# A 7x7 depthwise convolution whose taps are cut to the image, on one Trainium2 core

## Chip, core and metric

The kernel runs on one core of one Trainium2 chip. A core has TensorE (PE, matrix products into PSUM), VectorE (DVE, elementwise work), ScalarE (ACT, activation functions), GpSimd (POOL, here it issues the DMAs that add while they copy) and SyncE (SP, here it issues plain DMAs). Each engine works through its own queue in order, and they wait for one another by semaphores. The metric is the time of the device in microseconds for the whole program: the median of several executions. Profiles and traces are of one further execution.

## The reference

Eight images of 384 channels and 32 x 32 pixels, all float32, pass through two layers. Cut to what matters here:

```python
# layer 0: a transformer block on 1024 tokens of 384 channels
q, k, v = qkv(layernorm(xf))                       # 8 heads of 48
x1 = proj(softmax(q @ k.T * SCALE) @ v) + xf
x = x1 + fc2(gelu(fc1(layernorm(x1))))             # hidden 1536

# layer 1: a ConvNeXt block
y = conv_general_dilated(x, dw_w, padding=((3, 3), (3, 3)), feature_group_count=384)   # 7x7, depthwise
y = layernorm_over_channels(y + dw_b)
y = gelu(y @ w1 + b1)                              # 384 -> 1536
gx = sqrt(sum(y * y, over the pixels)); nx = gx / (mean(gx) + GRN_EPS)
y = grn_gamma * (y * nx) + grn_beta + y
out = x + y @ w2 + b2                              # 1536 -> 384
```

The depthwise convolution multiplies, for each of the 384 channels, 49 shifted copies of the image by 49 weights and adds them up. Outside the image the shifted copy is zero.

## The kernel before

The 384 channels are three tiles of 128 partitions, and an image of a tile is 1024 elements in each partition. The convolution is no matrix product here: a tap is one VectorE instruction, `acc = window * weight + acc`, on a tile with a border of three zeros all round (38 x 38). While it runs for image b - 1, TensorE is at the attention and the first MLP of image b. In the calls shown, `start_conv(b, ...)` begins the convolution of an image, and `conv_norm`, which runs inside the MLP of the next image, hangs its layer norm behind it.

```python
pad = const.tile([P, CT, HP, WP], F32, name="pad")          # 128 x 3 x 38 x 38, zeros at the border

def inner(ct):
    return pad[:, ct, PAD : PAD + H, PAD : PAD + W]

def convolution(acc, us, first=(), y0=0, y1=H, ready=tuple(range(CT)), taken=None):
    done = [0] * CT
    ct, n = None, 0
    taps = KS * KS - (HELPED if taken is not None else 0)    # HELPED = 7
    while min(done) < taps:
        left = [c for c in ready if done[c] < taps and not (taken and taken.get(c, 0) > flow.now)]
        # ... wait when there is none ...
        ct = min([c for c in left if c != ct] or left, key=lambda c: done[c])
        i = done[ct]
        dy, dx = divmod(i, KS)
        window = pad[:, ct, dy + y0 : dy + y1, dx : dx + W]
        dst = image(acc[:, ct, :])[:, y0:y1, :]
        tap = col("dww", ct * KS * KS + i)
        if i == 0:
            nc.vector.tensor_scalar(dst, window, tap, col("dwb", ct), ALU.mult, ALU.add)      # L978
        else:
            nc.vector.scalar_tensor_tensor(dst, window, tap, dst, ALU.mult, ALU.add)          # L980
        done[ct] += 1
        n += 1
        yield next((early for m, early in first if n <= m), us)
```

Seven of the 49 taps of a tile are taken over by ScalarE, which multiplies half an image at a time, and by GpSimd's DMAs, which add the product to `acc`. Meanwhile VectorE leaves that tile alone (`taken`).

```python
def help_convolution(acc, us, taken):
    yield 8.0
    for ct in reversed(range(CT)):
        taken[ct] = float("inf")
        for i in range(KS * KS - HELPED, KS * KS):
            dy, dx = divmod(i, KS)
            for h in range(2):
                # ... pauses while `quiet` ...
                t = three.tile([P, NH], F32, tag="res", bufs=4, name=f"tap_{ct}_{i}_{h}")
                y0 = dy + h * H // 2
                window = pad[:, ct, y0 : y0 + H // 2, dx : dx + W]
                tap = col("dww", ct * KS * KS + i)
                nc.scalar.mul(t.rearrange("p (h w) -> p h w", w=W), window, tap)              # L1001
                nc.gpsimd.dma_start(out=acc[:, ct, half(h)], in_=t, accum_op=ALU.add)         # L1002
                yield us
        taken[ct] = flow.now + 8.0
```

The order of the instructions is settled when the program is built. A small scheduler, `Flow`, counts how much time TensorE's matmuls should take (0.857 us for one of 512 columns) and, as that count passes, lets the other chains (convolution, layer norms, helpers) put their next instruction in their queues. What a chain yields is the number of such microseconds until its next step. So `us` is the pace at which taps are put among the other VectorE instructions, and `first` gives other paces for the first taps.

```python
start_conv(b, 1.65 if b == B - 2 else 1.7, (26, 2.2), (27, 9.0), (35, 4.4))     # in the loop; image 0: 1.6, (9, 1.65), (17, 4.4)
```

The last image has nothing left to hide behind, so it is split. Its MLP goes by halves of the image, and its convolution, which has no helpers and writes into the place of `wqkv`, starts on rows 0 to 12 when half of the image is ready, and then does rows 13 to 31:

```python
conv = convolution(last, 0.86 if h else 0.66, (), *rows, ready[h])
```

A layer norm over channels sums three tiles on VectorE, folds the two halves of the partitions with an adding DMA, sums over partitions with a matrix of ones on TensorE (the result stays in a PSUM bank), and subtracts the mean on VectorE, which frees the bank. The banks of this kind are four, in turn:

```python
ps_o = ctx.enter_context(tc.tile_pool(name="ps_o", bufs=4, space=PSUM))

# in layernorm(), cut:
nc.vector.tensor_tensor(a, src[:, 0, cols], src[:, 1, cols], ALU.add)                         # L413
nc.vector.tensor_tensor(a, a, src[:, 2, cols], ALU.add)                                       # L416
totals = yield from token_sums(a, ...)                                                        # L388 DMA; L380 or L394 matmul
nc.vector.scalar_tensor_tensor(to, total, -1.0 / C, of, ALU.mult, ALU.add)                    # L423, for each tile
# ... squares on ScalarE, summed (L434, L437) and added over partitions in the same way,
#     rstd by Ln (L447) and Exp (L448) on ScalarE ...
nc.vector.scalar_tensor_tensor(dst[:, ct, cols], dst[:, ct, cols], col(g, ct), rstd, ALU.mult, ALU.mult)   # L451
```

Of the kernel before, what the change touches and what calls it, by code (L numbers as in the profile page):

```python
# [52 lines left out]
B, C, H, W = 8, 384, 32, 32  # L53
# [6 lines left out]
KS, PAD = 7, 3  # L60
# [7 lines left out]
HELPED = 7  # L68
# [83 lines left out]
def block_kernel(  # L152
# [32 lines left out]
    def half(h):  # L185
        return slice(h * NH, (h + 1) * NH)
# [22 lines left out]
    pad = const.tile([P, CT, HP, WP], F32, name="pad")  # L209
# [14 lines left out]
    def col(name, i):  # L224
        at, width = VEC[name]
        assert i < width
        return vec[:, at + i : at + i + 1]

    def inner(ct):
        return pad[:, ct, PAD : PAD + H, PAD : PAD + W]  # L230

    def image(ap):
        return ap.rearrange("p (h w) -> p h w", h=H)
# [562 lines left out]
    def mlp(b, xt, xn, weights, tag, ln, rest, before_fc2=None, behind_ln=None):  # L796

        hid = one.tile([P, HT * N], F32, tag="big", name=f"hid_{b}").rearrange("p (m n) -> p m n", m=HT)
        e = [three.tile([P, 2, NH], F32, tag="p", name=f"fc2_e_{b}_{i}") for i in range(2)]
        wa = f"fc1_{tag}"  # L800
        flow.finish(ln)
        for m in range(HT):
            gelu_half(hid, m, 0, xn, weights, wa, f"fc1_{b}")
            if m == 3 and rest:
                rest()
                slow = 1.2 if b == 1 else 1.0
                ln = flow.spawn(layernorm(xt, xn, 1, eps0, "g2", f"ln2_{b}", True, slow=slow))
                behind_ln(ln)
        flow.finish(ln)
        for m in range(HT):  # L810
            gelu_half(hid, m, 1, xn, weights, wa, f"fc1_{b}")
            if m % CM == CM - 1:
                weights.used(wa, m // CM)
            if m in (3, 5):
                two_tiles = hid[:, m - 3 : m - 1, :]
                difference(e[(m - 3) // 2], two_tiles[:, :, half(0)], two_tiles[:, :, half(1)])
        if before_fc2:
            before_fc2()
        bias = lambda r: col("bfc2", r)
        by_thirds(xt, hid, e, True, weights, f"fc2_{tag}", bias, lambda r, n: pad_half(xt, r, n), f"fc2_{b}")  # L820
# [132 lines left out]
    def keep(b, xt):  # L953

        kept = dram.tile([C, N], F32, tag="kept", name=f"kept_{b}")
        nc.sync.dma_start(out=kept.rearrange("(c p) n -> p c n", p=P), in_=xt)
        return kept

    def convolution(acc, us, first=(), y0=0, y1=H, ready=tuple(range(CT)), taken=None):

        done = [0] * CT
        ct, n = None, 0
        taps = KS * KS - (HELPED if taken is not None else 0)
        while min(done) < taps:
            left = [c for c in ready if done[c] < taps and not (taken and taken.get(c, 0) > flow.now)]
            if not left:
                yield 1.0
                continue  # L970
            ct = min([c for c in left if c != ct] or left, key=lambda c: done[c])
            i = done[ct]
            dy, dx = divmod(i, KS)
            window = pad[:, ct, dy + y0 : dy + y1, dx : dx + W]
            dst = image(acc[:, ct, :])[:, y0:y1, :]
            tap = col("dww", ct * KS * KS + i)
            if i == 0:
                nc.vector.tensor_scalar(dst, window, tap, col("dwb", ct), ALU.mult, ALU.add)  # L978
            else:
                nc.vector.scalar_tensor_tensor(dst, window, tap, dst, ALU.mult, ALU.add)  # L980
            done[ct] += 1
            n += 1
            yield next((early for m, early in first if n <= m), us)

    def help_convolution(acc, us, taken):

        yield 8.0
        for ct in reversed(range(CT)):
            taken[ct] = float("inf")
            for i in range(KS * KS - HELPED, KS * KS):  # L990
                dy, dx = divmod(i, KS)
                for h in range(2):
                    if quiet:
                        while quiet:
                            yield 1.0
                        yield 3.0
# [9 lines that stand above are left out]
        taken.clear()  # L1006
# [188 lines left out]
    def load_kept(b, kept):  # L1195
        t = one.tile([P, CT, N], F32, tag="x", name=f"kept_{b}")
        nc.sync.dma_start(out=t, in_=kept.rearrange("(c p) n -> p c n", p=P))
        return t
# [13 lines left out]
    def after(first, chain, us=0):  # L1212
        if us:
            yield us
        while first is not None and first.gi_frame is not None:
            yield 1.0
        yield from chain
# [202 lines left out]
    def main():  # L1420
# [46 lines left out]
        def start_conv(b, us, *first):  # L1467
            acc = state["acc"] = one.tile([P, CT, N], F32, tag="acc", name=f"acc_{b}")
            taken = {}
            state["conv"] = flow.spawn(convolution(acc, us, first, taken=taken), paced=True)  # L1470
            state["help"] = flow.spawn(help_convolution(acc, 2.7, taken), paced=True)
# [53 lines left out]
        for b in range(B):  # L1525
            if b == 0:
                folding = flow.spawn(after(None, folds(weights), 8))
                preparing = flow.spawn(after(None, prepare(weights, False), 4))
                aside = flow.spawn(after(folding, prepare(weights, True), 4))
            q_and_k = qk(b, state["xn"], weights if b else None)  # L1530
            ln2, rest, xn = attention(b, xt, *q_and_k, (folding, aside) if b == 0 else ())
            if b < B - 1:
                mlp(b, xt, xn, weights, b, ln2, rest, lambda: next_norms(b), lambda ln: conv_norm(b, ln))
            else:
                acc = state["acc"]
                mlp_by_halves(b, xt, xn, weights, ln2, rest, last_convolution)
            kept[b] = keep(b, xt)
            if b + 1 < B:
                acc = state["acc"]
            if b == 0:  # L1540
                xt = load_x(b + 1, "x")
                flow.finish(preparing)
                start_conv(b, 1.6, (9, 1.65), (17, 4.4))
                next_values(1)
                continue
            if b < B - 1:
                xt = load_kept(b - 1, kept.pop(b - 1))
            flow.finish(state["norm3"])
            if b < B - 1:
                y, gx = grn_up(b - 1, acc, weights, b - 1)  # L1550
                start_conv(b, 1.65 if b == B - 2 else 1.7, (26, 2.2), (27, 9.0), (35, 4.4))
                scale = flow.spawn(grn_scale(b - 1, gx, weights, b - 1, y))
                next_values(b + 1)
                flow.finish(scale)
                quiet.append("w2")
                grn_down(b - 1, y, xt, weights, b - 1, b - 1)
                quiet.clear()
                xt = load_x(b + 1, "x")
            else:

                norm_b = flow.spawn(after(state["conv"], last_norm(LAST[1], 1.0)))
                norm_c = flow.spawn(after(norm_b, last_norm(LAST[2], 1.2)))
                y, gx = grn_up_straight(b - 1, acc, weights, b - 1)
                scale = flow.spawn(grn_scale(b - 1, gx, weights, b - 1))
                flow.finish(state["norm_a"])
                sums = small.tile([P, CT, HT], F32, tag="gx_last", bufs=1, name="gx_last")
                y_last = places()
                last_up(last, y_last, 0, sums, weights)
                flow.finish(scale)
                halves = lambda k, part: y[:, k, part]  # L1570
                blocks = [(r, half(n)) for r in range(CT) for n in range(2)]
                args = b - 1, halves, kept[b - 1], weights
                grn_down_straight(*args, b - 1, b - 1, blocks[:-1])
# [147 lines left out]
```

## Time and profile before

| | |
|---|---|
| time, median of 3 | 3316.8 us (3315.48 to 3319.44) |
| span of the profiled execution | 3315.9 us, 38765 instructions |
| TensorE busy | 3279.8 us |
| VectorE busy | 2511.5 us |
| ScalarE busy | 1604.1 us |
| taps of images 0 to 6 on VectorE | 861 at 1276 ns, and 21 first taps at 807 ns |
| taps of image 7 on VectorE | 144 at 644 ns and 144 at 844 ns, and 6 first taps |
| taps on ScalarE | 294 at 727 ns |

The profile gives each engine's busy time and the idle time ahead of its instructions, with what ended it (`<-` and the releaser). A wait view sums those by pair, a timeline puts the instructions in order of time, and a view by stretches gives busy time and the granted TensorE clock (1.00 is full speed) for any stretch. Each 32-bit product shows as two matmul records, so two passes of 512 columns make one product of the kernel.

### The profile page before, as it was taken

What the parts mean: (1) busy time and instruction counts of PE and PEld (TensorE: products, weight loads), DVE (VectorE), ACT (ScalarE), POOL (GpSimd) and SP (SyncE); (2) the same over time, 40 slices, a digit from 0 to 9 for tenths busy, and PEclk for the clock granted to TensorE, in tenths of its full rate; (3) what the DMA queues carried; (4) which work ended last, traced back from release to release, by engine and by line L of the source; (5) the groups of instructions that cost most, each with busy time, mean ns of one, the idle gap of its engine ahead of it and who ended that gap; (6) DMA issues with size and microseconds to landing.
All of it is one profiled execution on the core that took longest, in us unless ns stands there. A gap on an engine that the chain in (4) does not pass through costs nothing. (4 is left out here: it accounts for less than half of the span.)

```text
span 3315.9 us, 38765 instructions
## 1 busy us (share of the span) xinstructions
PE 3279.8 (99%) x14296; PEld 1415.0 (43%) x14296; DVE 2511.5 (76%) x3186; ACT 1604.1 (48%) x2194; POOL 484.2 (15%) x569
## 2 busy tenths in 40 slices
PE   8999999999999999999999999999999999999998
PEld 4344434443344433444344443444434443444455
DVE  4444897888867978679786798768886888879940
ACT  2542663447534375353652737526473355623541
POOL 2121210112110121101211022111220112100000
PEclk9999999999999999999999999999999999999999
DMA  5336732657244563537436373273742647333231
GB/s 197 112 106 147 150 68 71 156 115 150 56 104 135 137 127 58 131 106 172 84 58 148 103 187 70 58 179 84 175 78 50 180 106 160 63 74 89 69 95 43
DMA packets 199109, 368.73 MB, mean 111 GB/s; under 512 B 40768, under 2 KB 46784, under 8 KB 198528
## 3 DMA queue, kind: packets, MB, share of 16 engines
q0 software_dynamic: 80896, 158.63, 26.3%
q1 hardware_dynamic: 117728, 206.83, 20.7%
q8 instruction: 115, 1.88, 0.2%
q10 hardware_dynamic: 288, 0.71, 0.1%
q14 instruction: 82, 0.67, 0.1%
HBM read 187.03 MB, written 34.60 MB: 67 GB/s over the span
## 5 line engine op out<-in xcount | busy, mean ns | idle before, releaser
L980 DVE SCALAR_TENSOR_TENSOR acc<-pad,vec,acc 128x1024 f32<-128x1024 f32 x861 | 1069.3, 1276 | 20.1 <-DMA acc<-tap 15.5
L673 ACT ACTIVATE p<-s 128x1024 f32<-128x1024 f32 x512 | 523.8, 1023 | 278.5 <-PE s L664 270.1
L664 PE MATMUL s<-qk 48*64 48x512 f32 x4096 | 544.7, 593 | 0.8 <-ACT p L673 0.6
L684 PE MATMUL o<-p,v 64*64 64x512 f32 x4096 | 541.2, 591 | 0.0
L351 PE MATMUL fc<-xn,fc 128*128 128x512 f32 x1152 | 504.0, 596 | 4.8 <-DVE acc L423 4.8
L1002 POOL DMA_DIRECT2D acc<-tap x294 | 253.7, 884 | 1212.2 <-ACT tap L1001 747.9
L351 PEld LDWEIGHTS fc<-xn,fc 128*128 128x128 f32 x1152 | 219.2, 191 | 285.6 <-issue 275.7
L358 PE MATMUL fc_p<-hid,fc 128*128 128x512 f32 x728 | 318.6, 594 | 0.2 <-DMA hid<-hid 0.2
L370 ACT ACTIVATE hid<-fc,bfc_f 128x512 f32<-128x512 f32 x192 | 131.5, 686 | 348.0 <-PE fc L351 347.6
L684 PEld LDWEIGHTS o<-p,v 64*64 64x64 f32 x4096 | 165.5, 133 | 278.3 <-issue 266.7
L664 PEld LDWEIGHTS s<-qk 48*64 48x64 f32 x4096 | 161.2, 133 | 278.6 <-issue 220.5
L358 PE MATMUL o_p<-y,w 128*128 128x512 f32 x624 | 272.3, 593 | 0.0
L1051 DVE TENSOR_TENSOR y<-h,y 128x512 f32<-128x512 f32 x288 | 197.0, 690 | 90.8 <-PE h L358 76.2
L1001 ACT ACTIVATE tap<-pad,vec 128x512 f32<-128x512 f32 x294 | 210.9, 727 | 25.4 <-DMA acc<-tap 25.2
L358 PEld LDWEIGHTS fc_p<-hid,fc 128*128 128x128 f32 x728 | 137.2, 190 | 179.0 <-issue 166.5
L358 PE MATMUL h<-acc,w_A 128*128 128x512 f32 x432 | 207.3, 595 | 0.0
L980 DVE SCALAR_TENSOR_TENSOR wqkv<-pad,vec,wqkv 128x416 f32<-128x416 f32 (+1 forms) x288 | 193.5, 744 | 0.5
L358 PEld LDWEIGHTS o_p<-y,w 128*128 128x128 f32 x624 | 117.5, 190 | 150.6 <-issue 129.1
L790 ACT COPY pad<-x 128x512 f32<-128x512 f32 x48 | 30.2, 635 | 251.0 <-DVE x L856 187.0
L625 DVE TENSOR_TENSOR attn<-o,attn 128x512 f32<-128x512 f32 x64 | 44.1, 689 | 138.6 <-ACT attn L623 138.6
L549 DVE TENSOR_TENSOR qk<-qk,qk 128x512 f32<-128x512 f32 x168 | 111.5, 686 | 29.0 <-PE qk L358 20.0
L592 PE MATMUL v<-wqkv,xn 128*128 128x384 f32 x384 | 128.2, 491 | 0.0
(311 smaller groups left out, 3751.4 us busy)
## 6 DMA issues: line engine op xcount, KB each, us to landing
acc<-tap POOLq DMA_DIRECT2D x294, 256.0 KB, 3.5
w_A<-in_w SPq DMA_DIRECT2D x72, 384.0 KB
fc<-s_fc SPq DMA_DIRECT2D x91, 256.0 KB
hid<-hid POOLq DMA_DIRECT2D x42, 512.0 KB, 7.1
fc<-in_wfc SPq DMA_DIRECT2D x54, 384.0 KB
w<-s_w SPq DMA_DIRECT2D x78, 256.0 KB
y<-y POOLq DMA_DIRECT2D x36, 512.0 KB, 6.8
kept<-x SPq DMA_DIRECT2D x8, 1536.0 KB
```

Source lines behind the costliest of these rows:

```text
L351: nc.tensor.matmul(out=ps, lhsT=lhsT(k), rhs=rhs(k)[:, half(h)], start=(k == 0), stop=(k == nk - 1))
L358: nc.tensor.matmul(out=bank, lhsT=lhsT, rhs=rhs, start=k == 0, stop=k == len(pairs) - 1)
L370: nc.scalar.activation(dst, src, function, **kw)
L549: nc.vector.tensor_tensor(dst, bank, part, ALU.add)
L592: nc.tensor.matmul(out=ps[:, :C], lhsT=xn[:, k, t * P : (t + 1) * P], rhs=wv_sb[:, k, :], start=(k == 0), stop=(k == CT - 1),)
L664: nc.tensor.matmul(out=s[64 * i : 64 * i + 64, j, :], lhsT=kT[64 * j : 64 * j + HD, m, k0 : k0 + 64], rhs=qT[64 * j : 64 * j + HD, m, half ...
L673: nc.scalar.activation(p, s, AF.Exp)
L684: nc.tensor.matmul(out=outs[i][64 * j : 64 * j + 64, :], lhsT=v[keys, t, at : at + 64], rhs=p[keys, j, :], start=(t == 0), stop=(t == KT - 1),
L980: nc.vector.scalar_tensor_tensor(dst, window, tap, dst, ALU.mult, ALU.add)
L1001: nc.scalar.mul(t.rearrange("p (h w) -> p h w", w=W), window, tap)
L1002: nc.gpsimd.dma_start(out=acc[:, ct, half(h)], in_=t, accum_op=ALU.add)
L1051: nc.vector.tensor_tensor(dst, bank, part, ALU.add)
```

## The change

A tap only touches the part of the output whose source lies inside the image: the others would add zero. For that the first tap, which writes `acc` instead of adding, has to be one that covers the whole image, so the middle tap comes first. The taps on VectorE are cut to their rows and columns. The seven that ScalarE and the adding DMAs take over are now those that lose least by being cut: the one left of the middle and the six others of the middle column. They still work on whole windows with the zero border. So that taps of different size stand at fair distances, the pace is shared out by size (120 elements for the fixed part), with the total as before. Three paces are then set a little faster.

```diff
+    TAPS = [KS * PAD + PAD] + [i for i in range(KS * KS) if i % KS != PAD and i != KS * PAD + PAD - 1]
+    TAPS += [KS * PAD + PAD - 1] + [i for i in range(KS * KS) if i % KS == PAD and i != KS * PAD + PAD]
+
+    def inside(dy, dx, y0, y1):
+        rows = slice(max(y0, PAD - dy), min(y1, H + PAD - dy))
+        return rows, slice(max(0, PAD - dx), min(W, W + PAD - dx))
+
+    def size(dy, dx, y0, y1):
+        rows, cols = inside(dy, dx, y0, y1)
+        return 120 + (rows.stop - rows.start) * (cols.stop - cols.start)
 ...
         taps = KS * KS - (HELPED if taken is not None else 0)
+        shares = [size(*divmod(i, KS), y0, y1) for i in TAPS[:taps]]
+        shares = [taps * s / sum(shares) for s in shares]
 ...
             i = done[ct]
-            dy, dx = divmod(i, KS)
-            window = pad[:, ct, dy + y0 : dy + y1, dx : dx + W]
-            dst = image(acc[:, ct, :])[:, y0:y1, :]
-            tap = col("dww", ct * KS * KS + i)
+            share = shares[i]
+            dy, dx = divmod(TAPS[i], KS)
+            rows, cols = inside(dy, dx, y0, y1)
+            window = inner(ct)[:, rows.start + dy - PAD : rows.stop + dy - PAD, cols.start + dx - PAD : cols.stop + dx - PAD]
+            dst = image(acc[:, ct, :])[:, rows, cols]
+            tap = col("dww", ct * KS * KS + TAPS[i])
 ...
-            yield next((early for m, early in first if n <= m), us)
+            yield share * next((early for m, early in first if n <= m), us)
 ...                                                   # help_convolution
-            for i in range(KS * KS - HELPED, KS * KS):
+            for i in TAPS[KS * KS - HELPED :]:
 ...
-                start_conv(b, 1.65 if b == B - 2 else 1.7, (26, 2.2), (27, 9.0), (35, 4.4))
+                start_conv(b, 1.6 if b == B - 2 else 1.65, (26, 2.1), (27, 9.0), (35, 4.4))
```

## The prediction

> **What bounds the kernel now.** I read the busy shares first, then who waited for whom on TensorE, then the timeline around each TensorE wait, and last the groups of VectorE instructions with their shapes kept apart. The shares, from the page (engine, busy us, share, instructions):
>
> ```profile
> PE 3279.8 (99%) x14296; PEld 1415.0 (43%) x14296; DVE 2511.5 (76%) x3186; ACT 1604.1 (48%) x2194; POOL 484.2 (15%) x569
> ```
>
> TensorE is idle for 3315.9 - 3279.8 = 36.1 us in all. That is a ceiling of 1.1% on what a lighter VectorE (DVE) can return, since the change removes no matmul. A busy TensorE could hide short waits, so I checked one period of the middle: the sums of one image's second layer norm start at 1367.63, 1767.77 and 2167.91 us, 400.14 us apart. A 512-column pass takes 0.429 us in the trace (54 of them in 23.34 us, less the overlapping end of the last), and the matmuls that the program issues between two such points come to 396.2 us at that rate. The other 4 us are some ten switches to and from 64-row tiles at about 0.4 us each (the weight load behind such a switch stands 0.76 us after the one ahead instead of 0.24). So nothing is hidden: in the middle five images TensorE alone sets the pace. The stretches of 400 us say the same (start:end, length, then busy us of each engine, clock, DMA):
>
> ```profile
> 900.00:1300.00 400.00, 399.95 (x1745) 167.03 (x1744) 319.74 (x385) 204.15 (x266) 62.33 (x68) 1.00 0.51 114
> 1300.00:1700.00 400.00, 399.95 (x1745) 166.92 (x1744) 319.75 (x385) 204.16 (x266) 62.34 (x68) 1.00 0.51 114
> ```
>
> TensorE's waits by releaser (us in total, times, longest) are few:
>
> ```profile
> PE ln_sum L380 <- DVE ln_a L416: 11.8, 5, 5.9
> PE fc L351 <- DVE acc L423: 4.8, 1, 4.8
> PE ln_var L380 <- DVE ln_sq L437: 2.4, 1, 2.4
> PE h_last L1150 <- DVE wqkv L451: 1.6, 1, 1.6
> PE ln_var L394 <- DMA ln_sq<-ln_sq: 1.2, 2, 1.0
> ```
>
> By their places: 10.1 us of the first line lie before 30 us, long before the first convolution tap at 334 us. The rest of it (1.7), the 2.4 and the 1.6 lie together at 3183 to 3191 us. About 11 us more are the end after the last large matmul (3304.8 to 3315.9). One wait is left that convolution taps could cause: 4.8 us at 2974.4 to 2979.2. VectorE just ahead of it (start, us, line, operation, out<-in, count, idle before):
>
> ```profile
> 2936.72 15.81 DVE L980 SCALAR_TENSOR_TENSOR acc<-pad,vec,acc 128x1024 f32<-128x1024 f32 x12 [1.72 <-DMA acc<-tap]
> 2952.45 2.07 DVE L451 SCALAR_TENSOR_TENSOR xn<-xn,vec,ln_rstd 128x512 f32<-128x512 f32 x3
> ...
> 2958.54 0.70 DVE L978 TENSOR_SCALAR wqkv<-pad,vec 128x416 f32<-128x416 f32 x1 [0.70 <-ACT pad L790]
> 2959.28 10.28 DVE L980 SCALAR_TENSOR_TENSOR wqkv<-pad,vec,wqkv 128x416 f32<-128x416 f32 x15
> ...
> 2971.55 5.71 DVE L980 SCALAR_TENSOR_TENSOR wqkv<-pad,vec,wqkv 128x416 f32<-128x416 f32 x10
> 2977.17 3.67 DVE L423 SCALAR_TENSOR_TENSOR acc<-ln_sum,acc 128x512 f32<-128x512 f32 x6
> ```
>
> VectorE leaves a DMA wait at 2936.7 and then runs without a real pause: the last 12 taps of image 6 (counted from 0) and the first 27 instructions of image 7's convolution. Only then does it reach the subtraction of the mean (L423) that empties the PSUM bank TensorE needs. The bank holds sums that TensorE finished at about 2965.6. The third L423 ends at 2979.06, TensorE had run dry at 2974.39.
>
> The wait costs more than 4.8 us. Stretches with TensorE alone (length, busy us, clock, DMA):
>
> ```profile
> 2974.40:2979.10 4.70, 0.00 (x0) 0.94 0.01 2
> 2979.10:2985.20 6.10, 6.00 (x7) 0.50 0.00 0
> 2985.20:2991.20 6.00, 6.00 (x15) 0.99 0.24 66
> ```
>
> For 6.1 us after it the clock is halved: 7 passes 0.853 us apart instead of 0.429. That is 7 x 0.424 = 3.0 us more. The place costs 4.8 + 3.0 = 7.8 us.
>
> [...] the 4.81 us wait is followed by 6.1 us at 0.50, while the 1.01 us wait at 2881 leaves the clock at 1.00. [...]
>
> **The change part by part.** Tap shapes now:
>
> ```profile
> L980 DVE SCALAR_TENSOR_TENSOR acc<-pad,vec,acc 128x1024 f32<-128x1024 f32 x861 | 1069.3, 1276 | 20.1 <-DMA acc<-tap 15.5
> L980 DVE SCALAR_TENSOR_TENSOR wqkv<-pad,vec,wqkv 128x608 f32<-128x608 f32 x144 | 110.5, 844 | 0.0
> L980 DVE SCALAR_TENSOR_TENSOR wqkv<-pad,vec,wqkv 128x416 f32<-128x416 f32 x144 | 83.0, 644 | 0.5
> ```
>
> (844 - 644) / (608 - 416) = 1.042 ns for each element, and 844 - 608 x 1.042 = 210 ns fixed. 1024 elements then give 1277 ns, as measured.
>
> 1. Fewer elements. A tap's rows number 29, 30, 31, 32, 31, 30, 29 (sum 212), its columns likewise. ScalarE takes the six other taps of the middle column and the one left of the middle, which are full height or full width. VectorE keeps the middle tap and 41 taps with 180 x 212 - 31 x 32 = 37,168 elements instead of 41 x 1024 = 41,984. Saved: 4,816 x 1.042 ns = 5.0 us for each channel tile, 21 tiles, 105 us. The last image is split at row 13. Its taps have 85 rows of 91 and 127 of 133, which saves 2,364 and 2,868 elements, (2.46 + 2.99) x 3 = 16 us. VectorE falls by 121 us, to about 2,390 us (72%).
> 2. ScalarE's 294 products keep their padded windows of 128x512 and their 727 ns; the adding DMAs keep 256 KB. They cost what they cost before.
> 3. The pace of emission is scaled so that a convolution takes as long in the scheduler's own time as before, apart from 1.7 to 1.65 and 1.65 to 1.6. I counted, in the order of the built program, the tap work that stands ahead of every other VectorE instruction: it is never more than before, and per image it falls by up to 15 us. During images 2 to 6 the third layer norm's sums move ahead by four matmuls on TensorE (3.4 us).
> 4. Off the path: nearly all of the 121 us. In the middle the sums of that norm are folded by DMA from 955 us and read at 967 us, so there was slack there, and TensorE didn't wait anyway.
> 5. On the path: the wait at 2974 us. By the order, 10 taps with 8,850 elements stand where 12 stood; ScalarE and the DMAs ahead keep their order, so I keep the start at 2936.7. The old spacing was 15.81 / 12 = 1.318 us, of which 1.067 is elements: 10 x 0.251 + 8.850 x 1.042 = 11.7, 4.1 us less. Then 17 instructions with 5,648 elements instead of 16 with 6,656: spacing 0.685, so 0.252 beside the elements, gives 0.74 + 16 x 0.252 + 5.232 x 1.042 = 10.2 instead of 11.0, 0.8 less. Then 12 with 4,194 instead of 11 with 4,576 (here alternating tiles, about 0.56 apart): 6.0 instead of 6.2, 0.2 to 0.3 less. Sum 5.1 us: the third L423 ends at 2979.06 - 5.1 = 2973.9, half a microsecond before TensorE needs the bank. The 4.8 us go, and with them the 3.0 us of half clock. [...]
> 6. Kept: the waits at 3183 to 3191. There VectorE itself stood waiting (0.40 us) for TensorE's output block before the norm, and the norm keeps its place behind that block.
>
> Sum: 7.8 us, less 0.2 for the thin margin. 3316.8 - 7.6 = 3309.2, say 3309 us.
>
> **The rivals.** (a) Nothing is gained: the margin is half a microsecond, and if the short rows cost VectorE some cycles each, or the tap DMA lands later, the wait shrinks from 4.8 to 2 or 3 us and the half clock may stay: 3312 to 3316. For it: no row of the profile shows such a shape. Against it: today's source rows already lie 38 apart. (b) New waits in the middle: the sums that move ahead by 3.4 us may overtake their DMA, which lands some 5 us after 955; the slack of about 7 us falls to about 3 us. Were it lost, five images would pay perhaps 1 us each: 3310 to 3315. ScalarE now does that norm's squares ahead of one GELU, which holds a PSUM bank longer, but that bank is needed again only some 10 us later. (c) VectorE is the real bound and its 121 us count: then 3200. The 99% and the period rule this out.
>
> **Range and chances.** The first sum gives 3309; (a) and (b) reach to 3315.5; small waits (1.0 at 2881, 0.6 at 2788) that vanish by luck reach to 3304. Both edges are within 2% of 3316.8 (3250 to 3383), so same is all but sure: 0.985, with 0.005 for faster and 0.01 for slower.
>
> **What would show it.** Right: VectorE near 2,390 us busy, TensorE's total idle at 30 to 32 us, no wait of L351 for L423 near 2974, no stretch at clock 0.50 there, the cluster near 3180 unchanged, the period still near 400.1. Wrong: tap means off 210 + 1.042 per element; the wait still there; the period longer by a microsecond.

## The result and the profile after

The change takes the kernel from 3317.4 to 3304.2 us (medians of four executions each; those after lie between 3302.3 and 3306.6). The ratio is 0.9961, with a 95% interval of 0.9943 to 0.9978: 13.2 us, or 0.4%. The predicted time was 3309 us, in a range of 3304 to 3315.5; the result lies inside, close to its lower edge. So the question is where nearly 5 us more than expected came from.

The busy shares of the kernel after (engine, busy us, share of the span, instructions):

```profile
span 3304.7 us, 38767 instructions
PE 3274.8 (99%) x14296; PEld 1407.5 (43%) x14296; DVE 2396.4 (73%) x3186; ACT 1605.4 (49%) x2194; POOL 484.4 (15%) x569
```

VectorE has lost 115 us, TensorE's idle time has fallen from 36.1 to 3304.7 - 3274.8 = 29.9 us, and its *busy* time has fallen by 5.0 us with the same 14,296 matmuls. Of these, 3.0 us are the half clock after the wait, as foreseen; the others were not foreseen. The taps by shape, which the kernel before did not have (count, busy us, mean ns):

```profile
L998 DVE SCALAR_TENSOR_TENSOR acc<-pad,vec,acc 128x930 f32<-128x930 f32 x168 | 195.8, 1177 | 2.4 <-DMA acc<-tap 1.8
L998 DVE SCALAR_TENSOR_TENSOR acc<-pad,vec,acc 128x870 f32<-128x870 f32 x168 | 187.4, 1120 | 0.8
L998 DVE SCALAR_TENSOR_TENSOR acc<-pad,vec,acc 128x841 f32<-128x841 f32 x84 | 91.4, 1088 | 2.0 <-DMA acc<-tap 1.2
```

The formula 210 + 1.042 per element gives 1179, 1117 and 1086 ns, within 3 ns of these: a row of 29 to 31 elements costs nothing extra here. TensorE's waits by releaser (us in total, times, longest) no longer hold the line of L423:

```profile
PE ln_sum L380 <- DVE ln_a L416: 11.6, 5, 5.7
PE ln_var L380 <- DVE ln_sq L437: 2.4, 1, 2.4
PE h_last L1168 <- DVE wqkv L451: 1.6, 1, 1.6
```

The last taps of image 6 and the first of image 7 on VectorE, at the place where the kernel before waited (start, us, line, operation, out<-in, count, idle before; the shape is that of the first of the instructions counted):

```profile
2933.92 11.72 DVE L998 SCALAR_TENSOR_TENSOR acc<-pad,vec,acc 128x930 f32<-128x930 f32 x10 [1.76 <-DMA acc<-tap]
...
2952.39 9.48 DVE L998 SCALAR_TENSOR_TENSOR wqkv<-pad,vec,wqkv 128x290 f32<-128x290 f32 x16
...
2963.86 5.44 DVE L998 SCALAR_TENSOR_TENSOR wqkv<-pad,vec,wqkv 128x360 f32<-128x360 f32 x11
2969.22 3.67 DVE L423 SCALAR_TENSOR_TENSOR acc<-ln_sum,acc 128x512 f32<-128x512 f32 x6
```

and TensorE across the same point, in one stretch of 42 passes with no idle time ahead of it:

```profile
2968.79 18.42 PE L351 MATMUL fc<-xn,fc 128*128 128x512 f32 x42
```

The third L423 ends at about 2971.1 us. The first six passes of that stretch end at about 2971.5; the seventh needs the bank. The margin is 0.4 us, where 0.5 was reckoned. It is thinner than that, since passes overlap: the seventh starts at 2971.36, and in the kernel before its start stood 0.15 us behind the end of the third L423 (2979.05 and 2979.20). By that estimate 0.1 us was to spare.

**The account.** The same instruction, the first of an image's value matmuls (L592), dates both traces. Before, then after, two images running:

```profile
1080.42 4.03 PE L592 MATMUL v<-wqkv,xn 128*128 128x384 f32 x12
1480.57 3.71 PE L592 MATMUL v<-wqkv,xn 128*128 128x384 f32 x11
```

```profile
1081.18 3.07 PE L592 MATMUL v<-wqkv,xn 128*128 128x384 f32 x9
1480.76 3.71 PE L592 MATMUL v<-wqkv,xn 128*128 128x384 f32 x11
```

The period is 400.15 us before and 399.58 after. Taken from the first image to the last, the difference (after less before) builds up so:

| stretch | us |
|---|---|
| up to 331 us, before the first tap | +1.8 |
| images 1 to 6, about 0.56 us each | -3.4 |
| image 7's attention, to 2900 us | -1.2 |
| the wait at 2974 us with its half clock | -7.9 |
| the end | -0.4 |
| sum | -11.1 (spans 3315.87 and 3304.75) |

The first row cannot come from the taps, since none has run by then. In this one execution the clock stood at 0.57 from 318 to 322 us, after two waits of under half a microsecond (0.35 and 0.42 us), and the 30 passes from 318 us took 14.84 us; the trace before shows 1.00 there, and 13.14 us for the same passes. It is no mark of the change: of the traces below, that of experiment 8, with the old taps, has 14.84 us for them too, and that of experiment 4, with short ones, 13.14 us. Without this row the others come to 12.9 us, close to the 13.2 of the medians.

### The profile page after: what moved, and what is told of

It reads as the page before. It is cut to its first block, busy times and chain, and to the rows that moved or that the text cites. A ratio compares the mean times of both kernels' runs of the same rounds, so it can differ in the third digit from the quotient of the medians.

```text
span 3304.7 us, 38767 instructions
## 1 busy us (share of the span) xinstructions
PE 3274.8 (99%) x14296; PEld 1407.5 (43%) x14296; DVE 2396.4 (73%) x3186; ACT 1605.4 (49%) x2194; POOL 484.4 (15%) x569
## 4 chain that ended last, share of the span: by engine, by line
PE 89%; DMA 0%; issue 0%; DVE 0%; POOL 0%; ACT 0%; POOLq 0%; DVEq 0%
PE fc L351 15%; PE s L664 11%; PE o L684 11%; PE h L358 10%; PE fc_p L358 10%; PE o_p L358 9%; PE qk L358 6%; PE o L1124 4%; PE proj L606 3%; PE v L592 3%; PE h_last L1168 2%; PE h L338 2%; PE ln_var L394 1%; PE ln_sum L394 0%; PE ln_var L380 0%
## 5 line engine op out<-in xcount | busy, mean ns | idle before, releaser
L998 DVE SCALAR_TENSOR_TENSOR acc<-pad,vec,acc 128x870 f32<-128x870 f32 (+7 forms) x861 | 963.6, 1155 | 7.6 <-DMA acc<-tap 3.0
L673 ACT ACTIVATE p<-s 128x1024 f32<-128x1024 f32 x512 | 524.0, 1024 | 286.0 <-PE s L664 278.7
L998 DVE SCALAR_TENSOR_TENSOR wqkv<-pad,vec,wqkv 128x377 f32<-128x377 f32 (+24 forms) x288 | 177.3, 690 | 0.6
L592 PE MATMUL v<-wqkv,xn 128*128 128x384 f32 x384 | 129.3, 495 | 0.0
```

Source lines behind the costliest of these rows:

```text
L592: nc.tensor.matmul(out=ps[:, :C], lhsT=xn[:, k, t * P : (t + 1) * P], rhs=wv_sb[:, k, :], start=(k == 0), stop=(k == CT - 1),)
L673: nc.scalar.activation(p, s, AF.Exp)
```

## The experiments

Three theories are tested. **A**, the prediction's: one local wait at 2974 us is what the short taps remove, and VectorE's work elsewhere is off the path. **D**: from about 2937 to 3116 us VectorE itself is the bound, and the wait for L423 is only where its lateness is first felt. **F**: in the middle images VectorE is late by fractions of a microsecond at points that show no idle time. A letter that is not listed here stands for the rival which the same expectation describes. Edits are against the kernel after, unless the kernel before is named.

**1. The old paces of emission.**

```
-                start_conv(b, 1.6 if b == B - 2 else 1.65, (26, 2.1), (27, 9.0), (35, 4.4))
+                start_conv(b, 1.65 if b == B - 2 else 1.7, (26, 2.2), (27, 9.0), (35, 4.4))
```

> The changed kernel with the three paces of the kernel before (1.7, 1.65, 2.2). Theory A (what counts is the tap work that stands on VectorE ahead of the L423 that frees TensorE's PSUM bank, about 2974 us): in the order 12 taps with 10,620 elements stand there instead of 10 with 8,850. That is 2 x 0.251 + 1.770 x 1.042 = 2.35 us more against a margin of 0.4 us, so a wait of L351 for L423 of about 1.9 us comes back[...]: 3305 to 3309 us. Theory B (the gain is that of the new paces, short taps do nothing): 3314 to 3318, and the wait of 4.8 us is back. Theory C (the gain is that of less VectorE work anywhere, wherever it stands): as the changed kernel, 3302 to 3306, and no such wait.

Measured: 3306.4 us, ratio to before 0.9970 (0.9959 to 0.9981). TensorE at that place:

```profile
2973.50 15.96 PE L351 MATMUL fc<-xn,fc 128*128 128x512 f32 x36 [2.05 <-DVE acc L423]
```

The wait returns at 2.05 us but leaves the clock at 1.00, and the period stays 399.58 us. The short taps, with their order and shares, bring most of the gain at the old paces; the faster paces clear the rest of the wait. What that is worth in time is not told apart: the median is 2.2 us above the change's, but the executions of the two (3304.8 to 3309.2 and 3302.3 to 3306.6) overlap.

**2. Whole windows, with the new order and paces.**

```
-            window = inner(ct)[:, rows.start + dy - PAD : ..., cols.start + dx - PAD : ...]
-            dst = image(acc[:, ct, :])[:, rows, cols]
+            window = pad[:, ct, dy + y0 : dy + y1, dx : dx + W]
+            dst = image(acc[:, ct, :])[:, y0:y1, :]
```

> The changed kernel with its order of taps, its shares and its paces, but each VectorE tap on its whole window again (it adds zeros from the border). Theory A: 10 taps of 1024, 17 of 416 and 12 of 416 elements stand ahead of the L423, 1.5 + 1.4 + 0.8 = 3.7 us more than in the changed kernel, so a wait of about 3.3 us comes back; with or without the halved clock behind it, and with the small hidden waits of the middle images (period back from 399.6 to about 400.1 us): 3309 to 3316. Theory B (order, paces and helpers bring the gain, not the fewer elements): 3302 to 3306.

Measured: 3326.2 us, 1.0030 (1.0018 to 1.0042), slower than before. The total was missed, the wait was not:

```profile
PE ln_sum L380 <- DVE ln_a L416: 14.3, 8, 6.0
PE o_p L358 <- DVE y L856: 3.6, 12, 0.3
PE fc L351 <- DVE acc L423: 3.5, 1, 3.5
```

The miss is in the middle. The waits for L856 are new there, two in an image, and so are three more for ln_a; the period is 403.1 us in one image (1082.79 to 1485.90) and at least 401.6 in the others. All of these waits are for VectorE, so its slack in the middle was nearly nil: with whole windows the new order, shares and paces put more work ahead of what TensorE needs. Which of the three does it is not shown, since they were not tried apart; but without the fewer elements they lose time.

**3. Only the last image cut** (helpers and paces of the kernel before; `taken is None` holds for the last image alone).

```
+        cut = taken is None
+        order = TAPS if cut else list(range(KS * KS))
...              # short window and share only where cut; paces as before
```

> The kernel before, with the short taps, their order and their shares in the last image's convolution alone; images 0 to 6, their helpers and paces as before. Theory A: ahead of the L423 stand 12 whole taps of image 6 (15.8 us instead of 11.7), so the wait is 4.1 - 0.4 = 3.7 us instead of 4.8, with the halved clock behind it; the period stays 400.1: 3314 to 3317. Theory C (the last image is where VectorE is busiest, 3000 to 3100 us, so its taps bring most of the gain): 3304 to 3308.

Measured: 3315.1 us, 0.9996 (0.9987 to 1.0004). The wait shrinks to 3.74 us and is still followed by slow passes (clock 0.56 from 2979.5 to 2983 us). The period is 400.15 us, as before. The last image's cut alone brings next to nothing.

**4. All images cut but the last.** The same with `cut = taken is not None`, but with helpers and paces of the kernel after.

> The changed kernel with the last image's convolution as before (whole windows, old order). Theory A: 10 short taps of image 6, then 16 and 11 whole taps of image 7 stand ahead of the L423, 0.8 + 0.3 = 1.1 us more than in the changed kernel, so a wait of about 0.7 us comes back without a halved clock; the period stays 399.6: 3303 to 3307. Theory C: 3312 to 3316.

Measured: 3311.8 us, 0.9983 (0.9976 to 0.9989), 5 us above the range expected. The wait for L423 is 0.78 us, as expected, and the period 399.58. But the loss comes back later:

```profile
3109.45 18.51 PE L1174 MATMUL h_last<-wqkv,w_A 128*128 128x416 f32 x48 [2.49 <-DVE gmean L1191]
```

and VectorE's share of the stretch before it says why (window, length, busy us and instructions of PE, PEld, DVE, ACT and POOL, then clock and DMA):

```profile
2980.00:3110.00 130.00, 126.60 (x306) 56.27 (x305) 129.62 (x208) 53.62 (x77) 1.62 (x2) 1.00 0.26 72
```

VectorE works 129.62 of 130 us. What experiment 4 lets TensorE gain at 2974 us it waits off at 3107, because the taps of the last image still stand ahead of the mean (gmean, the `mean(gx)` of the reference). This is the first sign against A, which had no room for a loss behind 2974 us. Experiments 3 and 4 are each a part of the change, and they bring 1.9 and 5.1 us, while the whole brings 13.2.

**5. The sums in other banks** (the kernel before, taps untouched).

```
-            total = o_tile(f"{name}_{j}")[:, : cols.stop - cols.start]
+            if name.startswith(f"ln3_{B - 2}_sum"):
+                total = ps_s.tile([P, 2, NH], F32, tag="s", name=f"{name}_{j}")[:, 0, : cols.stop - cols.start]
+            else:
+                total = o_tile(f"{name}_{j}")[:, : cols.stop - cols.start]
```

> The kernel before, all its work and order kept, but the sums of the third norm of image 6 (the ones that the L423 at 2977 us empties) lie in PSUM banks of the pool that is idle in that stage, so TensorE needn't wait for that L423. Theory A (the wait for the bank is a local hold-up; take it away and its 4.8 us and the 3.0 us of half clock are saved): about 3309 us, 3306 to 3312. Theory D (from 2937 to about 3116 us VectorE is the bound, 129.1 of 130 us busy from 2980 on, and the bank is only where TensorE happens to feel it; TensorE then runs ahead by 7.8 us and waits for VectorE later, at the gmean of image 6 about 3110 us, for 5 to 8 us, perhaps with a halved clock): 3313 to 3320.

Measured: 3315.8 us, 0.9998 (0.9990 to 1.0007). TensorE no longer needs the bank that L423 empties. It waits at the next eviction instead (line numbers are higher by three in this kernel, so L426 is the former L423):

```profile
2971.28 7.89 PE L351 MATMUL fc<-xn,fc 128*128 128x512 f32 x18
2984.54 11.00 PE L351 MATMUL fc<-xn,fc 128*128 128x512 f32 x21 [5.37 <-DVE x L797]
```

VectorE's order shows that this eviction waits behind the same work:

```profile
2971.16 5.70 DVE L983 SCALAR_TENSOR_TENSOR wqkv<-pad,vec,wqkv 128x416 f32<-128x416 f32 x10
2976.79 3.67 DVE L426 SCALAR_TENSOR_TENSOR acc<-ln_sum,acc 128x512 f32<-128x512 f32 x6
2980.38 3.45 DVE L983 SCALAR_TENSOR_TENSOR wqkv<-pad,vec,wqkv 128x416 f32<-128x416 f32 x6
2983.75 0.73 DVE L797 SCALAR_TENSOR_TENSOR x<-fc,vec,x 128x512 f32<-128x512 f32 x1
```

5.4 us in place of 4.8, with the clock again at 0.50 after it. A falls: the bank was not the cause but the first place where a late VectorE is noticed. D holds, but it had the place wrong: the wait came one eviction on, at 2979 us, and not at gmean near 3110, where this run shows none.

**6. A faster pace for the second part of the last image.**

```
-                conv = convolution(last, 0.86 if h else 0.66, (), *rows, ready[h])
+                conv = convolution(last, 0.74 if h else 0.66, (), *rows, ready[h])
```

> The changed kernel with rows 13 to 31 of the last image paced at 0.76 instead of 0.86, so that the norm behind them begins ahead of the last output block but one instead of behind the last. VectorE has pauses of 1.0 to 1.5 us at each block there. Theory E (the waits of 1.7, 2.4 and 1.6 us at 3173 to 3180 us and the halved clock behind them, about 3.3 us, come from where the norm stands): the first two go and of the third about 1.6 is left without halved clock: 3296 to 3300 us. Rival (VectorE has no room at that pace, its blocks come late and TensorE waits for them or for gmean): 3302 to 3308.

> The same at 0.74: now the whole norm stands ahead of the last output block. Theory E: no wait is left there, 3294 to 3299 us. Rival: VectorE falls behind by about 1.5 us per output block and the norm comes no earlier than at 0.76: 3296 to 3302, or gmean comes late and holds TensorE up: 3302 to 3308.

Measured: 0.76 gives 3298.2 us, 0.9941 (0.9928 to 0.9955); 0.74 gives 3295.0 us, 0.9935 (0.9921 to 0.9949), the best of all versions and 9 us below the change itself. The stretch around the waits that the change had kept, first in the kernel after, then with 0.74:

```profile
3160.00:3180.00 20.00, 14.34 (x33) 5.92 (x31) 13.91 (x24) 3.88 (x7) 0.00 (x0) 0.88 0.31 85
3180.00:3200.00 20.00, 19.89 (x71) 15.14 (x72) 5.55 (x13) 13.90 (x34) 0.00 (x0) 0.86 0.33 83
```

```profile
3160.00:3180.00 20.00, 20.00 (x65) 11.97 (x64) 6.87 (x14) 9.74 (x23) 0.00 (x0) 1.00 0.44 121
3180.00:3200.00 20.00, 20.00 (x79) 14.59 (x78) 1.64 (x4) 18.83 (x54) 0.00 (x0) 1.00 0.46 123
```

The last taps are emitted earlier, so the last norm no longer stands behind the whole output block, and the three waits (1.70, 2.45 and 1.62 us) go with their half clock (0.50 from 3177 to 3183 us in the kernel after).

**7. The other seven taps helped**: the middle tap first and all others in their old order, so that ScalarE takes the bottom row again.

```
-    TAPS = [KS * PAD + PAD] + [i for i in range(KS * KS) if i % KS != PAD and i != KS * PAD + PAD - 1]
-    TAPS += [KS * PAD + PAD - 1] + [i for i in range(KS * KS) if i % KS == PAD and i != KS * PAD + PAD]
+    TAPS = [KS * PAD + PAD] + [i for i in range(KS * KS) if i != KS * PAD + PAD]
```

> The changed kernel with the seven taps of the last row (as in the kernel before) on ScalarE and the adding DMAs instead of the largest seven; VectorE then has 37,772 elements instead of 37,168 in 41 taps of a tile, 0.6 us more, 13 us in all. Theory A and D: ahead of the L423 stand 10 taps with 9,150 elements instead of 8,850, 0.3 us, within the margin of 0.4 us: as the changed kernel, 3302 to 3307 us. Rival (the choice of helpers is a part of the gain, by where VectorE waits for the adding DMAs): over 3308.

Measured: 3305.8 us, 0.9966 (0.9953 to 0.9978). VectorE is busy 2407.0 us, 10.6 more than after, and no wait for L423 appears. The time is not told apart from the change's: which seven taps are given away matters little. The period is 399.72 us, 0.14 more than after (experiment 8 shows where).

**8. Two taps later in the middle** (the kernel before).

```
-                start_conv(b, 1.65 if b == B - 2 else 1.7, (26, 2.2), (27, 9.0), (35, 4.4))
+                start_conv(b, 1.65 if b == B - 2 else 1.7, (24, 2.2), (25, 9.0), (35, 4.4))
```

> The kernel before with the first run of early taps of images 1 to 6 two shorter: 24 at a pace of 2.2 and the long pause after the 25th instead of 26 and the 27th, so that two taps less (2.6 us of VectorE) stand ahead of the first q and k tiles. No work is left out. Theory F (the period of 400.14 us holds about 0.56 us of TensorE waiting on a late VectorE around the end of the second layer's down product and the first q and k tile, shown as busy): the period falls to 399.6 to 399.8. Rival (the 0.56 us are something else, a memory or clock effect of the shorter rows): the period stays 400.1. The time as a whole says little: one whole tap more stands ahead of the L423 at 2977 us, so the wait there grows to about 6 us: 3313 to 3319.

Measured: 3316.5 us, 0.9998 (0.9989 to 1.0006). The wait for L423 grows to 6.07 us as expected. The period becomes 400.01 us, neither the 399.6 to 399.8 of F nor the 400.1 of its rival. The 0.56 us per image has two places, both in a stretch in which VectorE is busy 49.58 of 50 us (1115 to 1165, kernel before): 0.24 us in the 64 passes of the second layer's down product, and 0.32 us at the first query and key tile. In the kernel before they read

```profile
1120.19 27.87 PE L358 MATMUL o_p<-y,w 128*128 128x512 f32 x64
...
1156.47 3.92 PE L358 MATMUL qk<-xn,wqkv 128*128 128x512 f32 x8
```

in the kernel after

```profile
1120.95 27.63 PE L358 MATMUL o_p<-y,w 128*128 128x512 f32 x64
...
1157.00 3.60 PE L358 MATMUL qk<-xn,wqkv 128*128 128x512 f32 x8
```

and with two taps later

```profile
1121.74 27.87 PE L358 MATMUL o_p<-y,w 128*128 128x512 f32 x64
...
1158.03 3.60 PE L358 MATMUL qk<-xn,wqkv 128*128 128x512 f32 x8
```

The second place is thus VectorE's lateness, for putting two taps behind it removes it. Some 0.2 us come back in the next up product, at 1434 us, where a pass starts 0.06 us after the VectorE addition that it waits for.

The first place did not respond, but the starts of its passes show the same cause. This VectorE instruction of the kernel before makes the `y` that the down product reads next, and ends at 1139.15:

```profile
1137.93 1.22 DVE L856 TENSOR_TENSOR y<-y 128x1024 f32<-128x1024 f32 x1
```

The pass that it releases starts at 1139.20, 0.56 us behind the one ahead of it, and the next one 0.53 us later, where all others stand 0.43 apart: 0.24 us together. The profile shows no idle time, because a pass of 0.59 us still covers the start of the next. In the kernel after, that L856 ends 0.6 us before its pass starts, and the spacing stays 0.43. With two taps later it ends at 1140.70, 0.05 us ahead of its pass, with the same 0.56; in experiment 7 the spacing is 0.47 and 0.53, which is the 0.14 us of its period; in experiment 2 the same place shows the open waits for L856. So F holds for the whole 0.56 us.

**9. The faster pace without short taps** (the kernel before with `0.74 if h else 0.66`).

> The kernel before with rows 13 to 31 paced at 0.74 (what brought 9 us on the changed kernel). Theory D (from 2937 us on VectorE is the bound in the kernel before, so there is no room that a pace could use): 10 more taps stand ahead of gmean, 7.7 us, which adds to the 2.7 us by which it already comes after its matmul; TensorE waits about 7 us for it near 3110, with a halved clock, and that eats what the earlier norm saves: 3313 to 3322. Rival (the place of the norm is worth 9 us whatever the taps): 3306 to 3309.

Measured: 3319.2 us, 1.0004 (0.9995 to 1.0012). TensorE gets new waits, two of which are

```profile
3084.72 1.75 PE L380 MATMUL ln_var<-ln_sq,ones 128*128 128x416 f32 x2 [2.46 <-DVE ln_sq L437]
...
3125.38 2.36 PE L1150 MATMUL h_last<-wqkv,w_A 128*128 128x416 f32 x6 [1.34 <-DVE gmean L1167]
```

and VectorE works 59.76 of the 60 us from 3110 to 3170. So the gain of experiment 6 is not a better pace that anyone could have set: the short taps make the room, and the pace turns it into time.

## Why the prediction held, and where it fell short

**Steps 1 and 2, elements and helpers: right.** VectorE 2396.4 us against about 2,390. The taps themselves lost 121.9 us, as reckoned (1262.8 us in the three groups that the prediction shows, 963.6 + 177.3 after); the rest of VectorE's work took some 7 us more. The ten taps took 11.72 us against 11.7. ScalarE's busy time moved by 1.3 us, and experiment 7 shows that the choice of the seven is not what pays.

**Step 3, the paces: right in what they do, slightly low in worth.** With the old ones a wait of 2.05 us comes back (experiment 1). The sums that move ahead met no DMA too late.

**Step 5, the place at 2974 us: right in size.** 7.9 us against 7.8. With the half clock it is more than half of the gain.

**Step 6, the waits at 3183 to 3191: right.** They moved with the rest to 3172 to 3180 and kept their lengths (1.7, 2.4, 1.6 us). Experiment 6 shows that they were there for the taking.

**"So nothing is hidden: in the middle five images TensorE alone sets the pace": this step failed.** The count of 396.2 us of passes plus "some ten switches" of "about 0.4 us" was an estimate good to a microsecond, and it was used to exclude half a microsecond. The period fell by 0.56 us, 3.4 us over images 1 to 6. TensorE was recorded as busy throughout. The busy share could not show these waits, since a pass still covers the start of the next (experiment 8); the period near 400.1 us, named as a sign of being right, did not come. Experiment 4, with the short taps in those images alone, has the full 399.58; experiment 3, without them, has none of it. The range reached down to 3304 us for another reason, two small waits that might vanish by luck. One did, the 0.62 us at 2788; the other stayed. That the time lies inside the range, 0.2 us from its edge, is thus partly luck.

**Step 4, "Off the path: nearly all of the 121 us": right as a number, wrong as a map.** It put all the paying work ahead of 2974 us. Rival (c), that VectorE is the real bound, is false for the program but true from 2937 to about 3116 us:

```profile
2980.00:3110.00 130.00, 130.00 (x306) 57.47 (x305) 129.09 (x207) 51.92 (x71) 1.62 (x2) 0.98 0.25 69
3110.00:3170.00 60.00, 60.00 (x154) 28.76 (x154) 58.72 (x82) 24.36 (x67) 0.00 (x0) 1.00 0.32 93
```

That is the kernel before; the kernel after has

```profile
2980.00:3110.00 130.00, 130.00 (x319) 58.87 (x318) 124.19 (x209) 57.03 (x89) 1.62 (x2) 1.00 0.26 73
3110.00:3170.00 60.00, 60.00 (x147) 27.60 (x146) 52.38 (x78) 14.51 (x42) 0.00 (x0) 1.00 0.32 96
```

Before, both engines are full. The 4.8 us at 2974 kept TensorE late enough that VectorE could follow it from there on. Take the wait away without lightening the taps behind it, and VectorE is late at the next place (experiment 4, at gmean; experiment 5, one eviction on). The prediction came out right at this step because the change also lightens those taps, by 2,364 and 2,868 elements a tile, which the step had counted as worth nothing where they stand behind that point. That was luck.

**Rivals (a) and (b)** did not come. The margin of 0.4 us held in the run that was traced, with no wait at all; experiment 1 shows that the old pace leaves 2.05 us there. No new wait arose in the middle.

**Image 7's attention, 1.2 us.** Of these, 0.56 us are the same two places, at 2739 and 2757 us; 0.86 lie at the wait of 0.62 us for ScalarE at 2788, which the trace after does not show; and 0.2 are given back at 2882.

**Not settled:** why that wait for ScalarE is gone (experiments 5 and 8, with the old taps, don't list it either, so the short taps are not shown to be its cause), and why the clock halves near 320 us in some executions.

## What to carry to other kernels

A wait names the place where a late engine is felt, not the work that made it late: move the waiting somewhere else (another bank, a later read), and if it turns up at the next meeting point, the engine itself is the bound on that stretch. With one engine busy 99% of the span, look for stretches in which a second one is at 99% too: in this kernel, work taken from the second paid there. And room that is gained behind such a stretch is worth nothing until the order or pace of the work is set anew: here 9 us more than the change itself brought, and the same pace without the room brought nothing (3319.2 us).

## What the runs showed of the hardware

**TensorE's clock halved after some of its waits, and not after every one.** Waits of 5.37 (experiment 5), 4.81 (before) and 2.49 us (experiment 4) were each followed by a clock of 0.50, for at least 3.5, 6.1 and 2.5 us; one of 2.05 us (experiment 1) and one of 1.01 us (before) were followed by 1.00. In the kernel after, two waits of only 0.35 and 0.42 us, which ended at 315.5 and 317.0 us, were followed by 0.57 over the 4 us from 318. So the length of one wait alone did not decide it here; what else counted, no run tells. By an estimate from the 3.0 us lost in the 6.1 us after the wait of 4.81, each microsecond at half clock cost about another half.

**A tap with a scalar per partition took longer than a plain addition of as many elements, and most of the difference is in its fixed part.** In the trace after, an addition of 512 elements took 690 ns (L437, 30 of them) and one of 1024 took 1218 ns (L856, `y<-y`, 36 of them): by an estimate from these two, 162 ns fixed and 1.031 ns an element. Three taps of 512 elements took 743 ns each. The taps fit 210 ns + 1.042 ns an element from 290 elements (518 ns) to 992 (1247 ns), to within 2%. The run length of the rows, 29 to 32 elements, does not enter beyond that.
